# One group of small matmuls in place of two, three input buffers for it, and a later clamp in a convolution kernel

## Chip, core and metric

The kernel runs on one core of a Trainium2 chip. A core has five engines, each with its own queue that it works off in order: TensorE (PE in the profile; PEld is its weight load), VectorE (DVE), ScalarE (ACT), GpSimd (POOL) and SyncE (SP, which issues DMAs here). The metric is the time of one execution on the device in microseconds; smaller is better. All data are 32-bit floats.

## What is computed

The input x has 8 images of 256 channels and 64 x 64 pixels. Two layers follow each other, and each adds its result to its input. What matters here, cut from the reference:

```python
# layer 0, on the group-normalised x
x1, x2, x3 = _conv1x1(x, w1, b1), _conv1x1(x, w2, b2), _conv1x1(x, w3, b3)
...
h = jnp.concatenate([x1, x2u], axis=1)            # 320 channels: 32 + 9 shifts of 32
h = jax.nn.relu(_bn(h, bn1_g, bn1_b, bn1_m, bn1_v))
h = _conv1x1(h, cw1)                              # the inner conv: 320 -> 32
h = jax.nn.relu(_bn(h, bn2_g, bn2_b, bn2_m, bn2_v))
w = _conv1x1(h, cw2, cb2)                         # 9 weights per pixel and group
...
out = jnp.einsum('bgskhw,bgkhw->bgshw', x3u, w).reshape(B, OUT, H, W)
# layer 1, on the group-normalised result
att = jax.nn.softmax(jnp.einsum('bdn,bdkn->bnk', q, uk + upe[None]), axis=-1)
...
wts = jax.nn.softmax(wts, axis=2)                 # over 9 branches
hid = jax.nn.relu(_dwconv(xr, w1))
oc = _dwconv(hid, w2).reshape(b, kc2, C, h, w)
out_conv = jnp.sum(oc * wts.transpose(0, 2, 1, 3, 4), axis=1)
return rate1 * out_att + rate2 * out_conv
```

## The kernel before

An image is cut into 8 bands of 8 rows. The main loop runs over bands g; from g = 0 on it computes layer 1 of band g (image g // 8, band g % 8) and beside it pieces of layer 0 of bands that come later: the inner conv of band g + 11, the products of the nine pixel weights with the values (the taps) of band g + 10. Before that, in an opening of twelve bands, layer 0 runs alone. Layer 0 ends before the last bands: g = 0 to 52 contain an inner conv.

A band has 8 steps, s = 0 to 7, four for each half of the channels (ct = 0, 1; m = 0 to 3 in it). Step 6 is the seventh. Each step calls advance() six times. The order of instructions on each engine is the order in which the program issues them, and after(n, f) puts f off by n advances; a band is thus 48 places long, and step s begins at place 6s. Nothing else orders the work: an engine that has to wait holds up all that stands behind it in its queue.

In a step of layer 1 TensorE computes, among other things, scores (L750, tile sco, in even steps for two steps at once), the products of probabilities and values (L799, into the PSUM tile small), transposes (L787, tile ptp) and two groups of branch weights pf (L886). ACT turns each pf into exponentials ex (L891), and POOL adds up the ex tiles of a half band (L1106). There are three ex buffers, and pf, ptp, pv, pw, pk and pq share four PSUM buffers, so that a late addition on POOL keeps an exponential waiting, and that a matmul.

At a half band's end dynamic_sum closes the softmax over the nine branches: POOL adds the last two sums (L899, tile tot), adds 1 and limits the result to 1e37 (L902), VectorE takes the reciprocal in two halves through one buffer rec (L907), POOL multiplies (L908), then multiplies the depthwise result oc with it (L912) and adds that to xr (L913). oc itself is written by ACT (L879, in depthwise_end), at the end of step 3 or 7, and has two buffers.

The inner conv of a band (hidden_maps): ACT makes three inputs hid(0), hid(1), hid(2) of 512 columns (L424) in two buffers, at places 11, 16 and 25. The conv itself (L434) is twelve matmuls, four quarters of the band for each of the three inputs, each with 32 output rows; a 32-bit matmul leaves two records in the profile, so four matmuls are eight records. They go into a free part of the tile small: two inputs in step 4 (function one, place 24), whose sum ACT copies to SBUF (L446), and the third in step 6 (function two, place 36), after which VectorE adds the two (L450) and ACT applies scale, bias and ReLU (L441). In the opening (alone) the conv has a PSUM tile of its own, ph.

The taps: for each of nine taps VectorE makes a product prod (L483, two buffers, from the PSUM tile pw that L470 fills), and POOL adds it to xg (L491), 128 x 1024 elements each time.

Of the kernel before, what the change touches and what calls it, by code (L numbers as in the profile page):

```python
# [87 lines left out]
def conv_layers_kernel(ctx: ExitStack, tc: tile.TileContext, ins: dict, out: bass.AP):  # L88
# [102 lines left out]
    def layer1_loads():  # L191


        last = w1.tile([P, NCT, 1, C], F32, tag="oc", name="last")
        for f in late:
            f()
        nc.scalar.dma_start(out=last, in_=wfc_in[:, :, KK - 1 :])

        def first():
            nc.vector.tensor_scalar(wv, wv, rate1, None, ALU.mult)  # L200

        def difference(kt):
            nc.vector.tensor_sub(wfc[:, kt], wfc[:, kt], last[:, kt].to_broadcast([P, KK - 1, C]))

        return [first, lambda: difference(0), lambda: difference(1)]
# [205 lines left out]
    def hidden_maps(b, i, alone):  # L413

        im = images[b]
        hids = []
        h2 = h2n[i % 2][:, :, :W]

        def hidden(t):
            n = P if t == 0 else 96
            hid = w0.tile([P, R, W], F32, tag="hid", name=f"hid_{b}_{i}_{t}", bufs=2)
            nc.scalar.activation(  # L424
                hid[:n], im.x2[i][:n, t : t + R, :], AF.Relu, bias=bn1b[:n, t : t + 1], scale=bn1s[:n, t : t + 1]
            )
            hids.append(hid)

        def conv(home, first, last, start, stop):
            ph = home[:, 2 * P : 3 * P].rearrange("p (r c) -> p r c", r=SR)  # L430
            for t in range(first, last):
                n = P if t == 0 else 96
                for q in range(NQR):
                    nc.tensor.matmul(  # L434
                        ph[q * REL : (q + 1) * REL], c1[:n, t], hids[t][:n, q * SR : (q + 1) * SR],
                        start=(t == start), stop=(t == stop),
                    )
            return ph

        def relu(v):  # L440
            nc.scalar.activation(h2, v, AF.Relu, bias=bn2b, scale=bn2s)  # L441

        def one(home):
            ph = conv(home, 0, 2, 0, 1)
            after(1, lambda: hidden(2))
            after(2, lambda: nc.scalar.copy(h2, ph))  # L446

        def two(home):
            ph = conv(home, 2, 3, 2, 2)
            after(1, lambda: nc.vector.tensor_add(h2, ph, h2))  # L450
            after(3, lambda: relu(h2))

        hidden(0)
        after(3 if alone else 5, lambda: hidden(1))
        if alone:

            home = ps.tile([P, 4 * P], F32, tag="acc", name=f"ph_{b}_{i}")
            after(7, lambda: conv(home, 0, 2, 0, 2))
            after(8, lambda: hidden(2))
            after(12, lambda: after(4, lambda ph=conv(home, 2, 3, 0, 2): relu(ph)))  # L460
        return [two, one]

    def tap_weights(b, i, u, alone, at):

# [410 lines left out]

    def depthwise_end(b, i, ct, acc):

        oc = w1.tile([P, BAND], F32, tag="oc", name=f"oc_{b}_{i}_{ct}")
        nc.scalar.activation(oc, acc.rearrange("p r c -> p (r c)"), AF.Copy, scale=rate2)  # L879
        return oc  # L880

# [11 lines left out]
    def dynamic_sum(b, i, ct, ex, oc):  # L893

        tot = w1.tile([P, BAND], F32, tag="tots", name=f"tot_{b}_{i}_{ct}", bufs=1)
        xr = images[b].xr[i]

        engine = nc.vector if (b, i, ct) == (B - 1, NB - 1, NCT - 1) else nc.gpsimd
        engine.tensor_add(tot, ex[:, 1], ex[:, 0])  # L899


        engine.tensor_scalar(tot, tot, 1.0, 1.0e37, ALU.add, ALU.min)  # L902
        rec = w1.tile([P, BAND // 2], F32, tag="rec", name=f"rec_{b}_{i}_{ct}", bufs=1)

        def quotient(u):
            v = tot[:, u * BAND // 2 : (u + 1) * BAND // 2]
            nc.vector.reciprocal(rec, v)  # L907
            after(1, lambda: engine.tensor_mul(v, v, rec))  # L908

        def weigh():  # L910

            engine.tensor_mul(oc, oc, tot)  # L912
            engine.tensor_add(xr[:, ct], xr[:, ct], oc)  # L913
            if ct == NCT - 1:
                after(6, store)

        def store():
            nc.sync.dma_start(
                out=out[b].rearrange("(t p) n -> p t n", p=P)[:, :, i * BAND : (i + 1) * BAND], in_=xr
            )  # L920

        after(9, lambda: quotient(0))
        after(13, lambda: quotient(1))
        after(15, weigh)


    def beside(g, s):
# [96 lines left out]
    with tc.manual_schedule():  # L1024
# [21 lines left out]
        for g in range(-AHEAD, B * NB):  # L1046
            b, i = divmod(g, NB)
            for s in range(STEPS):
                ct, m = divmod(s, NT // 2)
                head, mid, end = beside(g, s)  # L1050
                if s == 1:
                    mid, maps = maps + mid, []
                steer(g, s)
                if g >= 0:
                    nm = f"{b}_{i}_{ct}_{m}"
                    weighted = []
                    if m % 2 == 0:
                        sco = score_tile(nm)
                        for e in range(2):
                            scores(b, i, ct, m + e, sco)  # L1060
                        small = small_tile(nm)
                        weighted, pending = weigh_steps(pending, small), []
                        if s == 0 and g + AHEAD < B * NB:
                            write = small_maps(*divmod(g + AHEAD, NB), small)
                            mid.append(lambda write=write: write((0,)))
                            maps.append(lambda write=write: write((1,)))
                        if s in (4, 6) and convs:
                            convs.pop()(small)
                        if before is not None:
                            pending.append((before[:-1], transposed(nm, before[-1])))  # L1070
                    prob, nmax = masked(nm, m, sco) if m % 2 == 0 else odd
                    for a, po in weighted:
                        add_values(*a, po)
                ahead = [f() for f in head]
                if g >= 0:
                    tot = exponentials(nm, prob, nmax)
                advance()
                for f in ahead:
                    if f:
                        f()  # L1080
                if g >= 0:
                    ex, exb = w1.tile([P, 2, BAND], F32, tag="ex", name=f"ex_{nm}", bufs=3), ex if m else None
                    branch_weights(b, i, ct, m, 0, ex)
                    if m % 2:
                        pending.append((before[:-1], transposed(nm, before[-1])))
                    if m in (0, 2):
                        todo = list(conv[0])
                    for _ in range(2):
                        todo.pop(0)()
                advance()  # L1090
                if g >= 0:
                    probabilities(prob, tot)
                rest = [f() for f in mid]
                advance()
                for f in rest:
                    if f:
                        f()
                if g >= 0:
                    for _ in range(2 if m % 2 == 0 else len(todo)):
                        todo.pop(0)()  # L1100
                    before = (b, i, ct, m, prob)
                advance()
                if g >= 0:
                    branch_weights(b, i, ct, m, 1, ex)
                    if exb is not None:
                        after(4, lambda ex=ex, exb=exb: nc.gpsimd.tensor_add(ex, ex, exb))  # L1106
                    if m == 1:
                        conv[1]()
                        conv = depthwise_middle(b, i, ct)
                    if m == NT // 2 - 1:  # L1110
                        oc = depthwise_end(b, i, ct, conv[1])
                        after(4, lambda a=(b, i, ct, ex, oc): dynamic_sum(*a))
                if s % 4 == 3 and 0 <= (g * NCT + ct + 1) < B * NB * NCT:
                    gn, cn = divmod(g * NCT + ct + 1, NCT)
                    conv = depthwise_begin(*divmod(gn, NB), cn)
                advance()
                for f in end:
                    f()
                if g >= 0 and m % 2 == 0:
                    odd = masked(f"{b}_{i}_{ct}_{m + 1}", m + 1, sco)  # L1120
                advance()
# [90 lines left out]
```

## Time and profile before

| what | value |
|---|---|
| median of 3 runs | 3856.01 us (3853.47 to 3856.48) |
| profiled execution | 3854.63 us |
| its span in the profile | 3852.8 us |
| granted TensorE clock, mean | 0.994 |
| HBM traffic | 127 GB/s over the span |
| inner conv, records of L434 in the bands | 1272, 270 to 297 ns each |
| limit L902 on POOL | 127 times, 1920 ns |
| limit L902 on VectorE (last half band) | once, 426 ns |
| copy L446, addition L450, ReLU L441 | 53 times each; 249, 280 and 483 ns |

An ordinary band takes 56.9 us, from one band's first score matmul to the next one's; the last image's bands take 49.6. In the timelines below a line has the start, the time, the engine, the source line, the operation, output and inputs, the shape and the count of merged instructions; in brackets stands how long the engine had been idle before it and what ended that wait. The lines with a stretch of time, such as 2405.50:2420.10, show its length and then, for each engine in the order PE, PEld, DVE, ACT, POOL, the busy time with the number of instructions, and last the clock, the share of the DMA engines and GB/s.

### The profile page before, as it was taken

What the parts mean: (1) busy time and instruction counts of PE and PEld (TensorE: products, weight loads), DVE (VectorE), ACT (ScalarE), POOL (GpSimd) and SP (SyncE); (2) the same over time, 40 slices, a digit from 0 to 9 for tenths busy, and PEclk for the clock granted to TensorE, in tenths of its full rate; (3) what the DMA queues carried; (4) which work ended last, traced back from release to release, by engine and by line L of the source; (5) the groups of instructions that cost most, each with busy time, mean ns of one, the idle gap of its engine ahead of it and who ended that gap; (6) DMA issues with size and microseconds to landing.
All of it is one profiled execution on the core that took longest, in us unless ns stands there. A gap on an engine that the chain in (4) does not pass through costs nothing.

```text
span 3852.8 us, 71646 instructions
## 1 busy us (share of the span) xinstructions
PE 3756.3 (97%) x24620; PEld 2109.9 (55%) x24620; DVE 3434.4 (89%) x7125; ACT 2809.2 (73%) x6770; POOL 3116.8 (81%) x2100
## 2 busy tenths in 40 slices
PE   6889999999999999999999999999999999999998
PEld 3445555555555555555555555555555555555554
DVE  6879999999999999899998999999999899978877
ACT  4457777777777777777777777777777777677776
POOL 4868888888897888888888888888888888855565
PEclk9999999999999999999999999999999999999999
DMA  8764544544444544544544544454544544232221
GB/s 247 210 177 128 142 118 129 151 126 118 133 135 131 145 123 115 148 135 127 136 116 142 142 125 120 126 149 125 136 115 117 138 119 114 74 97 78 79 67 37
DMA packets 438926, 490.14 MB, mean 127 GB/s; under 512 B 62016, under 2 KB 324256, under 8 KB 438304
## 3 DMA queue, kind: packets, MB, share of 16 engines
q1 hardware_dynamic: 421984, 469.79, 44.1%
q10 hardware_dynamic: 16576, 15.76, 1.3%
q8 instruction: 194, 3.18, 0.4%
q14 instruction: 172, 1.41, 0.1%
HBM read 343.76 MB, written 145.10 MB: 127 GB/s over the span
## 4 chain that ended last, share of the span: by engine, by line
PE 81%; POOL 10%; DVE 3%; DMA 2%; ACT 2%; issue 2%; SPq 1%; ACTq 0%; POOLq 0%; DVEq 0%
PE pf L886 39%; PE small L799 6%; PE ptp L787 6%; POOL xg L491 6%; PE pk L706 5%; PE pq L684 5%; PE sco L750 5%; PE p L375 5%; PE pv L601 5%; PE pw L470 2%; POOL ex L1106 2%; PE small L332 1%; DVE prod L483 1%; PE small L434 1%; DMA x<-x3n 1%
## 5 line engine op out<-in xcount | busy, mean ns | idle before, releaser
L886 PE MATMUL pf<-yp,c_wfc 128*128 128x512 f32 x4096 | 1916.8, 594 | 11.3 <-DVE prod L483 6.3
L491 POOL TENSOR_TENSOR xg<-xg,prod 128x1024 f32<-128x1024 f32 x549 | 1199.8, 2185 | 132.5 <-DVE prod L483 103.6
L886 PEld LDWEIGHTS pf<-yp,c_wfc 128*128 128x128 f32 x4096 | 739.6, 190 | 711.4 <-issue 654.7
L1106 POOL TENSOR_TENSOR ex<-ex,ex 128x1024 f32<-128x1024 f32 x384 | 908.8, 2367 | 68.5 <-ACT ex L891 65.0
L891 ACT ACTIVATE ex<-pf 128x512 f32<-128x512 f32 x1024 | 604.0, 590 | 347.9 <-PE pf L886 269.2
L843 DVE SCALAR_TENSOR_TENSOR acc<-yp,c_chan,acc 128x504 f32<-128x504 f32 (+3 forms) x1104 | 775.5, 702 | 63.2 <-ACT acc L834 42.8
L483 DVE SCALAR_TENSOR_TENSOR prod<-pw,c_par,x3q 128x1040 f32<-128x1040 f32 x576 | 732.7, 1294 | 107.9 <-PE pw L470 60.8
L869 DVE SCALAR_TENSOR_TENSOR acc<-hid,c_chan,acc 128x504 f32<-128x504 f32 (+3 forms) x1024 | 751.1, 733 | 18.1
L781 ACT ACTIVATE prob<-prob,tot 128x196 f32<-128x196 f32 x1024 | 412.9, 452 | 242.4 <-DVE tot L779 236.8
L772 ACT ACTIVATE prob<-prob,nmax 128x196 f32<-128x196 f32 x1024 | 458.2, 450 | 101.3 <-DVE nmax L764 101.2
L907 DVE RECIPROCAL rec<-tot 128x256 f32<-128x256 f32 x256 | 445.7, 1741 | 28.3 <-POOL tot L902 27.5
L789 ACT COPY pt<-ptp 112x512 f32<-112x512 f32 x511 | 295.9, 579 | 111.8 <-PE ptp L787 111.8
L764 DVE CUSTOM_DVE_ANT_0 prob<-sco,c_mask 128x196 f32<-128x196 f32 x1024 | 324.8, 355 | 31.0 <-PE sco L750 31.0
L787 PEld LDWEIGHTS ptp<-ident,prob 128*112 128x112 f32 x2044 | 227.3, 133 | 184.4 <-issue 132.7
L787 PE MATMUL ptp<-ident,prob 128*112 128x128 f32 x2044 | 319.5, 279 | 0.0
L908 POOL TENSOR_TENSOR tot<-tot,rec 128x256 f32<-128x256 f32 x254 | 185.8, 732 | 145.7 <-DVE rec L907 139.7
L799 PEld LDWEIGHTS small<-pt,vt 112*64 112x64 f32 x8144 | 258.6, 138 | 79.8 <-issue 60.5
L799 PE MATMUL small<-pt,vt 112*64 112x64 f32 x8144 | 294.2, 225 | 3.3 <-DMA vt<-vd 1.8
L601 PE MATMUL pv<-c_wv,yp 128*128 128x256 f32 x1056 | 253.5, 383 | 1.8 <-ACT yp L572 1.8
L902 POOL TENSOR_SCALAR tot<-tot 128x512 f32<-128x512 f32 x127 | 243.9, 1920 | 11.1
L470 PEld LDWEIGHTS pw<-h2n,c_c 128*128 128x128 f32 x1152 | 175.1, 191 | 139.9 <-issue 115.9
L375 PE MATMUL p<-xc,w3s 128*128 128x512 f32 x512 | 243.3, 598 | 0.0
(136 smaller groups left out, 4656.7 us busy)
## 6 DMA issues: line engine op xcount, KB each, us to landing
vt<-vd SPq DMA_DIRECT2D x512, 112.0 KB
x3q<-x SPq DMA_DIRECT2D x128, 264.0 KB
xc<-in_x SPq DMA_DIRECT2D x64, 512.0 KB
xg<-in_xg SPq DMA_DIRECT2D x64, 512.0 KB
yp<-x SPq DMA_DIRECT2D x128, 256.0 KB
xr<-x SPq DMA_DIRECT2D x64, 512.0 KB
out_x<-xr SPq DMA_DIRECT2D x64, 512.0 KB
xs<-in_x SPq DMA_DIRECT2D x57, 512.0 KB
```

What stands on the lines that cost most here:

```text
L483: nc.vector.scalar_tensor_tensor(prod[:, :, :RUN], pw[:, j, :RUN].unsqueeze(1).to_broadcast([P, SHARE, RUN]), par[:, PCB2 + k : PCB2 + k + 1],
L491: nc.gpsimd.tensor_add(im.xg[i], im.xg[i], rows(prod))
L601: nc.tensor.matmul(pv[:, g], yp[:, kt, r : r + 2].rearrange("p r c -> p (r c)"), wv[:, kt], start=(kt == 0), stop=(kt == NCT - 1),)
L772: nc.scalar.activation(prob[:, h, :NKEY], prob[:, h, :NKEY], AF.Exp, bias=nmax[:, h : h + 1], scale=-1.0, accum_out=tot[:, h : h + 1],)
L787: nc.tensor.transpose(ptp[:, h, ch], prob[:, h, ch * CHUNK : (ch + 1) * CHUNK], ident)
L799: nc.tensor.matmul(po[half[h], :, t * TQ : (t + 1) * TQ], im.vt[i + ch, m][:n, t, (2 * ct + h) * HD : (2 * ct + h + 1) * HD], pt[:n, h, ch ...
L843: nc.vector.scalar_tensor_tensor(o, yp[:, ct, ra + dr : rb + dr, ca + dc : cb + dc], chan[:, ct, CW1 + k : CW1 + k + 1], o, ALU.mult, ALU.add,
L869: nc.vector.scalar_tensor_tensor(o, hid[:, ra + dr : rb + dr, ca + dc : cb + dc], chan[:, ct, CW2 + k : CW2 + k + 1], o, ALU.mult, ALU.add,)
L886: nc.tensor.matmul(pf, wfc[:, kt, 2 * m + j, ct * P : (ct + 1) * P], images[b].yp[i][:, kt, PAD : PAD + R], start=(kt == 0), stop=(kt == N ...
L891: nc.scalar.activation(ex[:, j].rearrange("p (r c) -> p r c", r=R), pf, AF.Exp)
L907: nc.vector.reciprocal(rec, v)
L1106: after(4, lambda ex=ex, exb=exb: nc.gpsimd.tensor_add(ex, ex, exb))
```

## The change

The inner conv of a band is no longer split: all twelve matmuls are issued in step 6, accumulate in PSUM, and the ReLU reads them there one advance later. ACT's copy and VectorE's addition fall away. hid(2) is still made at place 25, but hid gets three buffers; to make room, oc (and the weights' tile that shares its tag) gets one. In the last band of each image, for the first half of the channels, the limit on tot is issued five advances later, the two reciprocals two and one advance later, and the product with oc one advance later. DMAs stay as and where they are.

```diff
-            hid = w0.tile([P, R, W], F32, tag="hid", name=f"hid_{b}_{i}_{t}", bufs=2)
+            hid = w0.tile([P, R, W], F32, tag="hid", name=f"hid_{b}_{i}_{t}", bufs=3)
...
-        def one(home):
-            ph = conv(home, 0, 2, 0, 1)
-            after(1, lambda: hidden(2))
-            after(2, lambda: nc.scalar.copy(h2, ph))
-
-        def two(home):
-            ph = conv(home, 2, 3, 2, 2)
-            after(1, lambda: nc.vector.tensor_add(h2, ph, h2))
-            after(3, lambda: relu(h2))
+        def inner(home):
+            ph = conv(home, 0, 3, 0, 2)
+            after(1, lambda: relu(ph))
...
+        else:
+            after(14, lambda: hidden(2))
+        return [inner]
...
-        oc = w1.tile([P, BAND], F32, tag="oc", name=f"oc_{b}_{i}_{ct}")
+        oc = w1.tile([P, BAND], F32, tag="oc", name=f"oc_{b}_{i}_{ct}", bufs=1)
...
-        engine.tensor_scalar(tot, tot, 1.0, 1.0e37, ALU.add, ALU.min)
+        def limit():
+            engine.tensor_scalar(tot, tot, 1.0, 1.0e37, ALU.add, ALU.min)
+
+        late = 2 if (i, ct) == (NB - 1, 0) else 0
+        if late:
+            after(5, limit)
+        else:
+            limit()
...
-        after(9, lambda: quotient(0))
-        after(13, lambda: quotient(1))
-        after(15, weigh)
+        after(9 + late, lambda: quotient(0))
+        after(13 + late // 2, lambda: quotient(1))
+        after(15 + late // 2, weigh)
...
-                        if s in (4, 6) and convs:
+                        if s == 6 and convs:
                             convs.pop()(small)
```

More of the change, by code (lines that the diff above doesn't have):

```diff
@@ L191, in layer1_loads @@
     def layer1_loads():
-        last = w1.tile([P, NCT, 1, C], F32, tag="oc", name="last")
+        last = w1.tile([P, NCT, 1, C], F32, tag="oc", name="last", bufs=1)
         for f in late:
@@ L460, in hidden_maps @@
             after(12, lambda: after(4, lambda ph=conv(home, 2, 3, 0, 2): relu(ph)))
-        return [two, one]
+        else:
+            after(14, lambda: hidden(2))
+        return [inner]
     def tap_weights(b, i, u, alone, at):
```

## The prediction

> **What bounds the kernel now.** I read the page's engine shares and chain of waits first, then one ordinary band (image 4, band 5, 2376.8 to 2433.7 us) cut into its four pairs of steps, then the timelines of single engines around the edited code.
>
> ```profile
> PE 3756.3 (97%) x24620; PEld 2109.9 (55%) x24620; DVE 3434.4 (89%) x7125; ACT 2809.2 (73%) x6770; POOL 3116.8 (81%) x2100
> PE 81%; POOL 10%; DVE 3%; DMA 2%; ACT 2%; issue 2%; SPq 1%; ACTq 0%; POOLq 0%; DVEq 0%
> 2391.40:2405.50 14.10, 14.10 (x89) 7.81 (x88) 13.82 (x28) 10.97 (x25) 12.68 (x9) 1.00 0.11 41
> 2405.50:2420.10 14.60, 14.60 (x115) 9.45 (x114) 13.77 (x26) 10.71 (x28) 14.28 (x8) 1.00 0.85 212
> ```
>
> TensorE (PE) looks like the only limit, but in steps 4 and 5 (the second of the two stretches, 2405.5 to 2420.1) GpSimd (POOL) is busy 14.28 of 14.60 us. So I followed POOL and those who wait for it.
>
> ```profile
> 2408.16 2.36 POOL L1106 TENSOR_TENSOR ex<-ex,ex 128x1024 f32<-128x1024 f32 x1
> 2410.48 4.44 POOL L491 TENSOR_TENSOR xg<-xg,prod 128x1024 f32<-128x1024 f32 x2
> 2414.88 2.37 POOL L1106 TENSOR_TENSOR ex<-ex,ex 128x1024 f32<-128x1024 f32 x1
> ...
> 2417.28 0.60 ACT L891 ACTIVATE ex<-pf 128x512 f32<-128x512 f32 x1 [1.91 <-POOL ex L1106]
> ...
> 2416.19 1.60 PEld L601 LDWEIGHTS pv<-c_wv,yp 128*128 128x128 f32 x8
> 2417.93 0.30 PEld L886 LDWEIGHTS pf<-yp,c_wfc 128*128 128x128 f32 x2
> ```
>
> POOL runs without a pause from 2395.40 (an xg addition of step 2) to 2417.25; the exponential of step 5 then starts at 2417.28, ends at 2417.88, and TensorE's next weight load (L886, second pf of step 5, whose PSUM buffer that exponential frees) comes 0.05 later. The load is some 0.1 later than the 0.02 it otherwise needs after the one before it, and its matmul starts only just on time. TensorE's own path has nothing left there: two chains tie. Matching every load with the wait that the built program gives it, this load stands 0.05 us behind ACT's exponential, and that 0.03 behind POOL, in 41 of the 53 bands that hold the changed conv; bands 3 (0.68) and 7 (0.12 to 0.16) of images 0 to 5 are the other twelve.
>
> The profile also holds a natural test. In image 6, band 5 is the first band with no inner conv; band 4 still has it:
>
> ```profile
> 3280.13 0.30 PEld L886 LDWEIGHTS pf<-yp,c_wfc 128*128 128x128 f32 x2 [0.90 <-ACT ex L891]
> ...
> 3334.01 0.30 PEld L886 LDWEIGHTS pf<-yp,c_wfc 128*128 128x128 f32 x2 [1.46 <-ACT ex L891]
> ...
> 3266.99 0.92 PE L750 MATMUL sco<-kb,qb 64*64 64x196 f32 x16
> 3282.27 0.92 PE L750 MATMUL sco<-kb,qb 64*64 64x196 f32 x16
> 3295.88 0.92 PE L750 MATMUL sco<-kb,qb 64*64 64x196 f32 x16
> ...
> 3320.88 0.92 PE L750 MATMUL sco<-kb,qb 64*64 64x196 f32 x16
> 3336.16 0.92 PE L750 MATMUL sco<-kb,qb 64*64 64x196 f32 x16
> ```
>
> Steps 4 and 5 last 15.28 in both bands: the conv's absence only lengthens the idle time from 0.90 to 1.46. Steps 6 and 7 do shrink, from 13.61 to 13.25 (the next score of band 5's successor is at 3349.40). Work in step 4 is hidden behind POOL; work in step 6 is paid in full.
>
> **What the Trainium skill says.** "Perfetto Trace Analysis", Optimization Strategy: the same gap repeating on an engine that should be saturated can mean that buffers ran out. Agrees: the late load of step 5 waits for a PSUM buffer, held up by the three ex buffers that POOL frees late. "TensorE: Matmul & The Clock Gate", Part 3, The mechanism: small matmuls at different tile positions overlap in the array. Agrees: eight L434 loads of 106 ns take 0.16 in all. "GPSIMD Engine Reference", 3.1: an elementwise addition is about twice as slow on GpSimd as on VectorE. Here the limit L902 is 1920 ns on POOL and 426 on VectorE, over four times.
>
> **The conv.** In the timeline of weight loads:
>
> ```profile
> 2392.23 1.01 PEld L799 LDWEIGHTS small<-pt,vt 112*64 112x64 f32 x32 [0.30 <-ACT ex L891]
> 2393.31 0.41 PEld L787 LDWEIGHTS ptp<-ident,prob 128*112 128x112 f32 x4
> ...
> 2406.39 1.01 PEld L799 LDWEIGHTS small<-pt,vt 112*64 112x64 f32 x32 [0.30 <-issue]
> 2407.47 0.38 PEld L434 LDWEIGHTS small<-hid,c_c 128*32 128x32 f32 x16
> 2408.04 0.40 PEld L787 LDWEIGHTS ptp<-ident,prob 128*112 128x112 f32 x4 [0.20 <-issue]
> ```
>
> From the end of L799 to the transposes L787: 0.07 without conv (step 2), 0.64 with 16 records (step 4), and 0.43 with 8 in step 6 (2421.93 to 2422.36). So the first piece costs 0.57, the second 0.36; eight records more are 0.21 to 0.22, the rest is the change of shape. After the change step 4 pays 0, step 6 pays 0.36 + 2 x 0.22 = 0.80: 0.44 more there, 0.57 less here, a net 0.13 per band for TensorE alone.
>
> In the 41 tied bands the 0.57 comes before the load that waits for POOL, and nothing in POOL's chain from step 2 to step 5 is edited or waits for the conv: it turns into idle time. The 0.44 comes after that load, and until step 5 of the next band I find no TensorE wait with less than 0.5 us to spare whose releaser moves against it: paid. 41 x 0.44 = +18.0. In band 3 the 0.57 fits into its 0.63: 6 x -0.13 = -0.8.
>
> With it go 53 ACT copies (249 ns, L446) and 53 VectorE additions (280 ns, L450). Both sit where their engine waits anyway: nothing. The ReLU L441 moves to just behind step 6's exponentials and delays the first ex of that step by 0.46; no TensorE load waits for that ex with under 0.7 to spare, and TensorE gets there 0.44 later: nothing.
>
> **Three hid buffers.** In the opening hid(2) waited for the first matmuls (ACT hid after PE ph: 10.4 us in 3 places). The chain passes that wait twice (54.99 and 199.88), 0.87 each with the issue: between -1.7 and 0; I take -0.9. In the bands the wait doesn't bind.
>
> **One oc buffer.** The write of oc (L879) now waits for POOL's addition L913 of the half band before. In the trace that addition ends before the write by 0.7 at the least in the first image, 1.1 or more later; example: 2377.88 against 2379.04. Step 6's extra 0.44 widens the narrow half. Zero; if it broke, behind it stand ACT's next acc copy L834 and the transposes' copy, a few tenths per band. The second wait is one queue instruction (17 ns for another of ACT's): nothing.
>
> **The limit in band 7** (images 0 to 5 have the taps beside it):
>
> ```profile
> 2532.03 1.92 POOL L902 TENSOR_SCALAR tot<-tot 128x512 f32<-128x512 f32 x1
> 2534.03 4.43 POOL L491 TENSOR_TENSOR xg<-xg,prod 128x1024 f32<-128x1024 f32 x2
> ...
> 2536.24 1.30 DVE L483 SCALAR_TENSOR_TENSOR prod<-pw,c_par,x3q 128x1040 f32<-128x1040 f32 x1 [0.50 <-POOL xg L491]
> ...
> 2535.90 0.40 PEld L787 LDWEIGHTS ptp<-ident,prob 128*112 128x112 f32 x4 [0.20 <-issue]
> 2537.60 0.30 PEld L886 LDWEIGHTS pf<-yp,c_wfc 128*128 128x128 f32 x2 [1.29 <-DVE prod L483]
> ```
>
> POOL's order becomes sum, xg, limit, xg, xg, ex, both products with the reciprocals. The first xg starts at 2531.94 and frees the prod buffer at 2534.1; the last prod then runs 2534.2 to 2535.4. Transposes to pf take 0.38 elsewhere, here 1.70: 1.32 lost. TensorE would want the load at 2536.28, shifted by -0.22 (what this band keeps of 0.57: 0.10 of slack and the 0.12 by which loads run ahead) and +0.44: 2536.50, later than prod. The stall goes: 6 x (-0.22 + 0.44 - 1.32) = -6.6. What is late next: the second reciprocal needs the one rec buffer and so waits for the first product, behind two xg and an ex, about 2543.5 instead of 2540.26. Behind it on VectorE are step 7's masks (some 0.7 later than 2545.07), then the exponentials; TensorE needs them for the transposes at 2553.7. Zero, at worst the 1.1 gained. In images 6 and 7 no taps stand beside it: zero.
>
> **Sum:** 18.0 - 0.8 - 6.6 - 0.9 = +9.7 on the profiled execution's 3854.63 (span 3852.8 and 1.8 around it) is 3864.3. The median stands 1.38 above that execution, so 3865.7.
>
> **Rivals.** (1) Not slower: POOL's chain ends 0.57 or more earlier in the ordinary bands, because a part of it is started by something that the change brings forward, and TensorE alone sets the time: 53 x -0.13, 6 x -1.32 and -0.9, -15.7, so 3840.3. For it speaks TensorE's 81% of the chain; against it the two bands of image 6. (2) The gain of band 7 only moves to another wait (the reciprocal behind POOL): 18.0 - 0.8 + 6 x 0.22 - 0.9 = +17.6, so 3873.6. For it: VectorE is 89% busy and in order; against: four microseconds to spare. (3) Half of the 0.44 disappears, because loads run ahead of matmuls after the stall: -9.0, so 3856.7. Against: in image 6 step 6 gave back its whole 0.36.
>
> **Chances.** Forecast 0.64, rival 1 0.13, rival 2 0.13, rival 3 0.10. The forecast's own range is 3861 to 3871: 0.05 per tied band is 2 us, the opening 0.9, band 7 another 1, and runs before differ by 3. The range 3856 to 3875 adds rivals 2 and most of 3; rival 1 stays out. A difference of 0.2% (7.7 us) is what measurement can tell from none: above 3863.7 lie three quarters of the forecast and rival 2, 0.61; below 3848.3 rival 1, 0.13; the rest 0.26.
>
> **What would show it.** Right: the load of step 5 idle 0.5 to 0.7 behind ACT's exponential in ordinary bands, steps 4 and 5 as long as before (14.5), steps 6 and 7 at 14.05 instead of 13.61, L434 in one group of 24, and no stall behind prod in band 7. Wrong: steps 4 and 5 shorter by half a microsecond, or ACT's oc waiting for POOL.

## The result, and the profile after

| | before | after |
|---|---|---|
| median | 3854.88 us (10 runs, 3849.93 to 3858.0) | 3865.21 us (10 runs, 3859.89 to 3869.82) |
| ratio | | 1.0026, 95% interval 1.0016 to 1.0035 |
| profiled execution (span) | 3854.63 (3852.8) us | 3869.82 (3867.7) us |
| mean granted TensorE clock in the profile | 0.994 | 0.991 |

The change makes the kernel 10.3 us slower. The profiled execution of after is the longest of its ten; the spans of the ten go from 3857.7 to 3867.7 us at mean clocks of 0.994 to 0.991. So the 14.9 us between the two profiles' spans are not yet the change's price: 1.8 of them lie in the opening, which does not repeat well (see the last section), and 13.1 behind it. Single stretches are compared instead, from one score matmul to the next, and the opening is left aside.

From the page of after: the engines' shares, the chain of waits by engine, and the group of the branch-weight matmuls (busy time and mean ns of one, then the idle time before them):

```profile
PE 3764.2 (97%) x24620; PEld 2115.7 (55%) x24620; DVE 3422.6 (88%) x7072; ACT 2804.8 (73%) x6717; POOL 3116.7 (81%) x2100
...
PE 61%; POOL 23%; DVE 6%; ACT 5%; issue 3%; DMA 2%; SPq 0%; ACTq 0%; POOLq 0%; DVEq 0%
...
L882 PE MATMUL pf<-yp,c_wfc 128*128 128x512 f32 x4096 | 1920.5, 595 | 16.7 <-ACT ex L887 15.6
```

The shares of busy time hardly move. The chain does: TensorE falls from 81% to 61%, POOL rises from 10% to 23%, although POOL does exactly the same work as before (2100 instructions, 3116.7 us). The chain passes through POOL because in most bands a matmul now really waits for it: the 16.7 us of idle time before pf are nearly all ended by ACT's exponential, whereas before it was 11.3 us, of which VectorE's prod ended 6.3. That 20 points of the chain move while the time moves by 0.3% fits two chains that end almost together.

An ordinary band (image 4, band 5) by pairs of steps, first steps 4 and 5, then 6 and 7; columns are length, then PE, PEld, DVE, ACT, POOL, clock, DMA. Before:

```profile
2405.54:2420.07 14.53, 14.53 (x111) 9.41 (x111) 13.73 (x26) 10.64 (x28) 14.21 (x8) 1.00 0.85 212
2420.07:2433.68 13.61, 13.61 (x90) 6.93 (x89) 12.43 (x27) 8.03 (x20) 13.37 (x11) 1.00 0.51 130
```

After:

```profile
2415.12:2429.66 14.54, 14.22 (x96) 9.04 (x95) 13.64 (x26) 10.43 (x27) 14.22 (x8) 1.00 0.86 212
2429.66:2443.71 14.05, 14.05 (x106) 7.37 (x105) 12.87 (x27) 8.11 (x20) 13.81 (x11) 1.00 0.49 131
```

Steps 4 and 5 lost the sixteen matmul records of the conv's first piece (the window's edges make it 15 here) and kept their length: PE is busy 14.22 of 14.54 us where it had been busy throughout. Steps 6 and 7 gained sixteen records and 0.44 us. The timelines of the weight loads, ACT and POOL of after show both places:

```profile
2424.46 2.37 POOL L1109 TENSOR_TENSOR ex<-ex,ex 128x1024 f32<-128x1024 f32 x1
...
2426.87 0.60 ACT L887 ACTIVATE ex<-pf 128x512 f32<-128x512 f32 x1 [2.49 <-POOL ex L1109]
...
2425.19 1.60 PEld L597 LDWEIGHTS pv<-c_wv,yp 128*128 128x128 f32 x8
2427.52 0.30 PEld L882 LDWEIGHTS pf<-yp,c_wfc 128*128 128x128 f32 x2 [0.72 <-ACT ex L887]
...
2430.51 1.01 PEld L795 LDWEIGHTS small<-pt,vt 112*64 112x64 f32 x32 [0.30 <-issue]
2431.59 0.60 PEld L434 LDWEIGHTS small<-hid,c_c 128*32 128x32 f32 x24
2432.38 0.41 PEld L783 LDWEIGHTS ptp<-ident,prob 128*112 128x112 f32 x4 [0.20 <-issue]
```

The load of step 5 stands idle for 0.72 us and starts 0.05 after the exponential ends, which itself waited for POOL's addition of the ex tiles. In bands 1, 2, 4 and 5 of images 0 to 5 this load idles 0.68 to 0.73, in band 6 1.02 to 1.06, in band 0 0.35 to 0.36. The conv is one group of 24 records; from the end of the L795 loads (2431.52) to the transposes it is 0.86. In step 6 of before it was 0.43:

```profile
2420.92 1.01 PEld L799 LDWEIGHTS small<-pt,vt 112*64 112x64 f32 x32 [0.30 <-issue]
2422.00 0.16 PEld L434 LDWEIGHTS small<-hid,c_c 96*32 96x32 f32 x8
2422.36 0.40 PEld L787 LDWEIGHTS ptp<-ident,prob 128*112 128x112 f32 x4 [0.20 <-issue]
```

Over all bands, after minus before by pairs of steps ("tied" are the bands in which POOL's chain and TensorE's path end together in step 5, or POOL's ends later):

| bands | steps 4, 5 | steps 6, 7 |
|---|---|---|
| 40 tied bands (images 0 to 5 without 3 and 7; image 6, 0 to 3) | 0.00 (-0.07 to +0.02; band 0 of images 1 to 6 -0.18 to +0.09, of image 0 -0.45) | +0.44 |
| band 3 of images 0 to 5 | -0.58 | +0.43 |
| band 7 of images 0 to 5 | -0.22 | -0.87 |
| image 6, band 4 | -0.56 | +0.45 |
| image 6, band 5 | -0.59 | 0.00 |
| last score matmul to the end of the span | | 25.46 before, 28.42 after |

Steps 0 to 3 stay within 0.01, but for band 0 of image 0, right behind the opening: there steps 2 and 3 are 1.43 longer, and the band as a whole is 1.2 longer. Band 7 alone gains in steps 6 and 7; there the limit was moved. The timelines of after around its step 6 (image 4):

```profile
2541.12 1.27 POOL L895 TENSOR_TENSOR tot<-ex 128x512 f32<-128x512 f32 x1
2542.34 2.18 POOL L487 TENSOR_TENSOR xg<-xg,prod 128x1024 f32<-128x1024 f32 x1
2544.61 1.92 POOL L899 TENSOR_SCALAR tot<-tot 128x512 f32<-128x512 f32 x1
...
2544.56 1.30 DVE L479 SCALAR_TENSOR_TENSOR prod<-pw,c_par,x3q 128x1040 f32<-128x1040 f32 x1 [1.65 <-POOL xg L487]
...
2546.59 0.40 PEld L783 LDWEIGHTS ptp<-ident,prob 128*112 128x112 f32 x4 [0.20 <-issue]
2546.97 0.30 PEld L882 LDWEIGHTS pf<-yp,c_wfc 128*128 128x128 f32 x2
```

The limit now stands behind the first xg. The product ends at 2545.86, over 1 us before the load of L882 comes up, and that load no longer carries a bracket: it follows the transposes after 0.38, where it had stood idle for 1.29 behind prod.

The last line of the table is the very end of the program. Before, VectorE and POOL there:

```profile
3826.37 1.75 DVE L907 RECIPROCAL rec<-tot 128x256 f32<-128x256 f32 x1
3828.36 0.36 DVE L764 CUSTOM_DVE_ANT_0 prob<-sco,c_mask 128x196 f32<-128x196 f32 x1 [0.25 <-PE sco L750]
...
3831.58 1.73 DVE L907 RECIPROCAL rec<-tot 128x256 f32<-128x256 f32 x1
...
3833.39 0.73 POOL L908 TENSOR_TENSOR tot<-tot,rec 128x256 f32<-128x256 f32 x1 [2.14 <-DVE rec L907]
...
3836.78 4.79 POOL L1106 TENSOR_TENSOR ex<-ex,ex 128x1024 f32<-128x1024 f32 x2
```

After:

```profile
3840.30 0.36 DVE L760 CUSTOM_DVE_ANT_0 prob<-sco,c_mask 128x196 f32<-128x196 f32 x1 [1.91 <-PE sco L746]
...
3841.89 1.74 DVE L910 RECIPROCAL rec<-tot 128x256 f32<-128x256 f32 x1
3843.55 1.46 DVE L865 SCALAR_TENSOR_TENSOR acc<-hid,c_chan,acc 128x504 f32<-128x504 f32 x2
...
3845.04 1.53 DVE L865 SCALAR_TENSOR_TENSOR acc<-hid,c_chan,acc 128x504 f32<-128x504 f32 x2
3846.47 1.75 DVE L910 RECIPROCAL rec<-tot 128x256 f32<-128x256 f32 x1
...
3848.30 0.73 POOL L911 TENSOR_TENSOR tot<-tot,rec 128x256 f32<-128x256 f32 x1 [3.86 <-DVE rec L910]
...
3851.69 4.77 POOL L1109 TENSOR_TENSOR ex<-ex,ex 128x1024 f32<-128x1024 f32 x2
...
3851.78 0.69 ACT L875 ACTIVATE oc<-acc,c_rowp 128x512 f32<-128x512 f32 x1 [0.15 <-POOL xr L916]
```

Before, the first reciprocal ran while VectorE waited for the last scores; the masks then waited only 0.25. After, the masks wait 1.91 with nothing in that gap, the first reciprocal comes behind them, and one more pair of depthwise operations stands before the second one. The last score matmul starts at 3827.38 before and 3839.31 after; the second reciprocal follows it by 4.20 before and by 7.16 after, POOL's last two additions by 9.40 and 12.38. These 3.0 us reach the end undiminished: the closing operations on VectorE begin when POOL's last addition is done. It is also the one place where ACT's oc waits for POOL (0.15).

### The profile page after: what moved, and what is told of

Its sections match the earlier page's. It is cut to its first block, busy times and chain, and to the rows that moved or that the text cites. A ratio compares the mean times of both kernels' runs of the same rounds, so it can differ in the third digit from the quotient of the medians.

```text
span 3867.7 us, 71658 instructions
## 1 busy us (share of the span) xinstructions
PE 3764.2 (97%) x24620; PEld 2115.7 (55%) x24620; DVE 3422.6 (88%) x7072; ACT 2804.8 (73%) x6717; POOL 3116.7 (81%) x2100
## 4 chain that ended last, share of the span: by engine, by line
PE 61%; POOL 23%; DVE 6%; ACT 5%; issue 3%; DMA 2%; SPq 0%; ACTq 0%; POOLq 0%; DVEq 0%
PE pf L882 29%; POOL xg L487 12%; POOL ex L1109 7%; PE small L795 5%; PE sco L746 4%; PE p L375 4%; PE ptp L783 4%; PE pq L680 3%; PE pk L702 3%; DVE prod L479 2%; PE pv L597 2%; PE pw L466 1%; PE small L332 1%; POOL oc L915 1%; ACT ex L887 1%
## 5 line engine op out<-in xcount | busy, mean ns | idle before, releaser
L882 PE MATMUL pf<-yp,c_wfc 128*128 128x512 f32 x4096 | 1920.5, 595 | 16.7 <-ACT ex L887 15.6
L882 PEld LDWEIGHTS pf<-yp,c_wfc 128*128 128x128 f32 x4096 | 739.2, 190 | 725.3 <-issue 661.2
L795 PEld LDWEIGHTS small<-pt,vt 112*64 112x64 f32 x8144 | 258.5, 138 | 79.6 <-issue 60.5
L795 PE MATMUL small<-pt,vt 112*64 112x64 f32 x8144 | 294.0, 225 | 3.4 <-DMA vt<-vd 1.8
L899 POOL TENSOR_SCALAR tot<-tot 128x512 f32<-128x512 f32 x127 | 243.9, 1920 | 11.1
L357 POOL COPY x<-x 32x8 f32<-32x8 f32 x64 | 12.1, 189 | 296.4 <-ACT x L347 296.4
```

The source lines that it names most:

```text
L795: nc.tensor.matmul(po[half[h], :, t * TQ : (t + 1) * TQ], im.vt[i + ch, m][:n, t, (2 * ct + h) * HD : (2 * ct + h + 1) * HD], pt[:n, h, ch ...
L882: nc.tensor.matmul(pf, wfc[:, kt, 2 * m + j, ct * P : (ct + 1) * P], images[b].yp[i][:, kt, PAD : PAD + R], start=(kt == 0), stop=(kt == N ...
```

## The experiments

Theory: in steps 2 to 5 of an ordinary band POOL's chain and TensorE's own path end together, so taking work out of step 4 gives nothing, and work put into step 6 is paid in full. The first rival: the two places are alike, and the loss comes from something else in the change (buffers, the single oc, VectorE's order). The second: the limit moved in band 7 only shifts its stall.

### The parts of the change

**The joined conv without the later limit** (edit of after):

```diff
-        late = 2 if (i, ct) == (NB - 1, 0) else 0
+        late = 0
```

> The changed kernel without the later limit: one conv group in step 6, three hid buffers, one oc buffer. Theory (POOL's chain hides step 4, step 6 is paid): each ordinary band keeps its +0.44, bands 3 their -0.14; in band 7 of images 0 to 5 the stall of 1.31 is back and swallows what the conv adds there, so band 7 is as before; the end is as in the kernel before. 39 x 0.44 - 6 x 0.14 - 0.7 (bands 4 and 5 of image 6, as measured) = +15.6 against before: about 3870.5. Rival (the conv alone only saves TensorE 0.13 a band, and the loss came from the limit): 3848.

Measured: 3868.05 us (5 runs, 3866.44 to 3869.71), ratio to before 1.0037 (1.0024 to 1.0049). By bands: +0.44 in the tied ones, -0.58 and +0.43 in band 3, about -0.22 and +0.20 in band 7, the two bands of image 6 as in after, the end at 25.46 as before. So the loss of steps 6 and 7 and the gains of image 6 belong to the conv and its buffers, which are taken alone below; the end does not. The medians of the series differ by 15.2, where 15.6 was expected.

**The later limit alone, in images 0 to 5** (edit of before, the later limit as in the change but under a condition):

```diff
+        late = 2 if (i, ct) == (NB - 1, 0) and b < B - 2 else 0
```

> The kernel before with the later limit alone, and only in images 0 to 5, where taps stand beside it. Theory: the stall of 1.31 behind prod goes in six bands and nothing else moves: -7.9 against before, about 3847. Rival (the stall only moves to the reciprocals and step 7's masks): 0 to -2, about 3854.

Measured: 3846.38 us (20 runs), ratio 0.9982 (0.9976 to 0.9989). Steps 6 and 7 of the six bands are 1.30 to 1.34 shorter, no other band moves by more than 0.06, the end takes 25.47. The rival of the shifted stall falls: the wait is gone, and nothing takes its place.

**The later limit alone, in all eight images** (edit of before):

```diff
+        late = 2 if (i, ct) == (NB - 1, 0) else 0
```

> The kernel before with the later limit in all eight images' last bands. Theory: six bands with the taps gain 1.32 each (7.9, as when the limit alone is moved there), and the last half band's end comes 3.0 later by the second reciprocal behind POOL's first product: -4.9, 3848.6; the stretch from the last score matmul to the end goes from 25.5 to 28.4. Rival (the longer end needs the single oc buffer or the joined conv): the end stays at 25.5 and the time is 3846.

Measured: 3848.7 us (21 runs), ratio 0.9988 (0.9982 to 0.9995). The six bands gain 1.30 to 1.34 again, and the end takes 28.42. So the 3.0 us at the end come from the limit's edit by itself; neither the single oc buffer nor the conv is needed. The number was as expected, but the mechanism named there was not: in this run and in after VectorE is busy without a pause from the first reciprocal to the second, and POOL's first product (in after 3843.71 to 3844.44) is long done. The second reciprocal is late by its place in VectorE's order, not by the rec buffer.

**The whole change with the later limit in images 0 to 5 only** (edit of after):

```diff
-        late = 2 if (i, ct) == (NB - 1, 0) else 0
+        late = 2 if (i, ct) == (NB - 1, 0) and b < B - 2 else 0
```

> The changed kernel with the later limit left out in the last two images. Theory (in the last half band the later reciprocals delay POOL's last two ex additions and with them the end): the last stretch, from the last score matmul to the end, takes 25.4 again instead of 28.4, and nothing else changes: -3.0 against the changed kernel, about 3862. Rival (the longer end in the profile is TensorE's slower clock there, half speed for 17.5 us instead of 10.5): still 28, about 3865.

Measured: 3861.47 us (18 runs), ratio to before 1.0021 (1.0014 to 1.0028). All bands but the very first are as in after, the end takes 25.46 instead of 28.42. The medians differ from after's by 3.7, the two ratios by 0.0005 (1.9 us); the 3.0 of the end lies between. The rival named for this run falls as well: TensorE's mean clock over the last stretch is lower here (0.77) than in before (0.83), and both take 25.46.

**The buffers alone** (edit of before: three hid buffers, one oc buffer; the weights' tile that shares oc's tag gets one too):

```diff
-            hid = w0.tile([P, R, W], F32, tag="hid", name=f"hid_{b}_{i}_{t}", bufs=2)
+            hid = w0.tile([P, R, W], F32, tag="hid", name=f"hid_{b}_{i}_{t}", bufs=3)
...
-        oc = w1.tile([P, BAND], F32, tag="oc", name=f"oc_{b}_{i}_{ct}")
+        oc = w1.tile([P, BAND], F32, tag="oc", name=f"oc_{b}_{i}_{ct}", bufs=1)
```

> The kernel before with the buffer edits alone: three hid buffers, one oc buffer; conv split as before, limit as before. Theory: nothing in any band (the oc write never waits), 0 to 1.7 less in the opening: 3852 to 3853.5. Rival (the single oc buffer costs): ACT's oc is idle behind POOL's addition in half bands, a few tenths in each of 64 bands, 3865 or more.

Measured: 3854.39 us (13 runs, 3847.26 to 3859.1), ratio 1.0003 (0.9994 to 1.0011). That is 0.9 above the range that was expected, well within an interval that is 6.5 us wide. Band 0 of images 1 to 5 moves by +0.06 to +0.08 in steps 4 and 5, 0.4 in all, and band 0 of image 0 by +1.2; no other by more than 0.06. The same first band moves by -0.9 to 0.0 in the runs that leave the buffers alone and by -1.5 to +1.2 in those that have them, so its +1.2 is not put down to the buffers. They are not the loss of steps 6 and 7 or of the end. Whether the opening gains up to 1.7 can't be told.

### The tie with POOL, from both sides

**Without the first piece** (edit of before; step 4 then has no conv and no copy on ACT):

```diff
-            ph = conv(home, 0, 2, 0, 1)
             after(1, lambda: hidden(2))
-            after(2, lambda: nc.scalar.copy(h2, ph))
```

> The kernel before without the first piece of the inner conv: step 4's matmuls and ACT's copy are left out, the third input is added to what stood in the buffer. Theory: 0.57 of TensorE's work per band is free under POOL's chain, except in band 3 (-0.57, six times): the idle time of step 5's load grows by 0.57 and the time falls by 3.4 to 4.5, about 3850. Rival (TensorE's work counts wherever it stands): 53 x -0.57 = -30, about 3824.

Measured: 3851.06 us (13 runs), ratio 0.9996 (0.9987 to 1.0004). That is 2.4 less than before, where 3.4 to 4.5 was expected; the interval goes from 5.0 less to 1.5 more. The 16 records cost 0.57 us on TensorE, yet behind band 0 of image 0 only band 3 (-0.57) and steps 4 and 5 of band 7 (-0.22, which its stall in step 6 takes back) get shorter. The same load of step 5 in the timeline of weight loads, and steps 4 and 5 of the band, in this kernel:

```profile
2418.20 0.30 PEld L884 LDWEIGHTS pf<-yp,c_wfc 128*128 128x128 f32 x2 [0.69 <-ACT ex L889]
```

```profile
2405.84:2420.34 14.50, 14.21 (x95) 9.04 (x95) 13.64 (x26) 10.43 (x27) 14.18 (x8) 1.00 0.89 213
```

Work taken from step 4 turns into 0.69 of idle time, just as after the change.

**Without the second piece** (edit of before; step 6 then has no conv and no addition on VectorE):

```diff
-            ph = conv(home, 2, 3, 2, 2)
-            after(1, lambda: nc.vector.tensor_add(h2, ph, h2))
```

> The kernel before with the third input's four matmuls and VectorE's addition left out of step 6 (the branch weights then lack that part of the conv's sum; step 4's piece stays). Theory (step 6 pays in full, step 4 is covered by POOL): 0.36 less in steps 6 and 7 of every one of the 53 bands, with at most 0.2 of it lost in band 7 of images 0 to 5, 47 to 53 x 0.36 = 17 to 19 us: about 3836. Rival (the two places are alike, both are hidden behind POOL or in TensorE's slack): as the kernel before without step 4's piece, 3851. Rival (the 0.36 is mostly the change of shape and comes back at the next group): 3845.

Measured: 3839.13 us (5 runs), ratio 0.9962 (0.9949 to 0.9974). Steps 6 and 7 are 0.35 to 0.36 shorter in 46 bands, in all 53 but the six bands 7, which stay, and band 4 of image 0 (0.14). The sum of that, about 17, is at the lower end of the expected 17 to 19, a little more than the 14.4 between the medians and inside their interval (10 to 20). Steps 6 and 7 of the same band as above:

```profile
2404.90:2418.15 13.25, 13.25 (x81) 6.77 (x81) 12.10 (x26) 8.03 (x20) 13.01 (x11) 1.00 0.48 129
```

Half as many records as in the run before, and several times the gain: the places are not alike.

**POOL relieved, in after**: the copy of the last band's rows into kb (L670, 0.54 us) stands in POOL's chain of steps 2 to 5; for the second half of the channels it goes to ACT.

```diff
-                nc.gpsimd.tensor_copy(kb[:, : 2 * PAD], im.kb[i - 1, ct][:, R:])
+                (nc.scalar.copy if ct else nc.gpsimd.tensor_copy)(kb[:, : 2 * PAD], im.kb[i - 1, ct][:, R:])
```

> The changed kernel with one copy of POOL's chain (kb rows of the second channel half, 128x420, 0.53 us, step 2) moved to ACT. Theory: POOL's chain from step 2 to step 5 is 0.5 shorter, the idle time of step 5's load falls from 0.7 to about 0.2, and the 39 tied bands become 0.45 to 0.5 shorter: -18, about 3847. Rival (what was lost is TensorE's own work in step 6): unchanged, 3865.

Measured: 3847.32 us (17 runs), ratio to before 0.9983 (0.9976 to 0.999), where after has 1.0026. Steps 4 and 5 of the tied bands are 0.43 to 0.53 shorter than in after (those of band 0 of an image are not: no such copy stands in its chain), steps 6 and 7 as in after. The load and the windows of the same band:

```profile
2411.75 0.30 PEld L882 LDWEIGHTS pf<-yp,c_wfc 128*128 128x128 f32 x2 [0.21 <-ACT ex L887]
```

```profile
2399.86:2413.89 14.03, 14.03 (x96) 9.04 (x95) 13.65 (x26) 10.41 (x27) 13.79 (x7) 1.00 0.83 209
```

The idle time falls from 0.72 to 0.21, what POOL gave up.

**POOL relieved, in before** (the same edit of before):

> The kernel before with the kb copy of step 2 on ACT. Theory (before, POOL's chain and TensorE tie, so a shorter chain brings nothing in ordinary bands): only band 6 (-0.33), band 7's stall (-0.48, six times each) and bands 4 and 5 of image 6 (-0.5 each) gain: -5.9, about 3847. Rival (POOL's chain sets every band): 41 x -0.48, about 3833.

Measured: 3846.83 us (21 runs), ratio 0.9984 (0.9977 to 0.999). The ordinary bands gain nothing (0.00); the 6.7 us come from band 6 (-0.41), band 7 (about -0.48), bands 4 and 5 of image 6 (-0.76 and -0.64) and the end (-0.3): 6 x 0.89 + 1.4 + 0.3 = 7.0. In the ordinary band the load now has no wait at all, and the steps are as long as ever:

```profile
2413.75 0.41 PEld L886 LDWEIGHTS pf<-yp,c_wfc 128*128 128x128 f32 x2
```

```profile
2401.47:2416.00 14.53, 14.53 (x112) 9.50 (x111) 13.74 (x26) 10.65 (x28) 14.29 (x7) 1.00 0.84 201
```

That settles the tie. Relieving TensorE alone gives nothing (no first piece), relieving POOL alone gives nothing (this run), relieving both gives half a microsecond in every tied band whose chain holds the copy (the run before this one).

### A better place

**The joined conv in step 4**, where POOL covers 0.57 of its 0.80 (edit of the version with the limit in images 0 to 5):

```diff
-            after(14, lambda: hidden(2))
+            after(11, lambda: hidden(2))
...
-                        if s == 6 and convs:
+                        if s == 4 and convs:
```

> The changed kernel with the one conv group in step 4 instead of step 6 (hid(2) three advances earlier), and the later limit only in images 0 to 5. Theory: the group of 24 costs 0.80 in step 4, where TensorE just ties with POOL's chain, and step 6 pays nothing: +0.22 and -0.36 against the kernel before, -0.14 in an ordinary band; where TensorE idled for POOL in step 5 (band 0 by 0.1, band 6 by 0.33) the 0.22 is free; the stall of band 7 is gone. 53 x -0.14 - 2.0 - 7.9 = -17 against before, about 3837. Rival (the place doesn't matter, only the group's size): as with step 6, 3862.

Measured: 3839.72 us (5 runs, 3834.86 to 3843.07), ratio 0.9968 (0.9955 to 0.998). Against before, steps 4 and 5 are 0.20 to 0.22 longer in ordinary bands and steps 6 and 7 are 0.36 shorter; band 0 of the later images loses 0.3 to 0.6 in steps 4 and 5, which was not foreseen and has not been traced. It makes up about 3 us, what the run stays behind the 17 that were expected. The load of step 5 has no wait, and the band's two windows are:

```profile
2394.44:2409.18 14.74, 14.74 (x119) 9.72 (x118) 13.73 (x26) 10.79 (x28) 14.42 (x8) 1.00 0.84 209
2409.18:2422.43 13.25, 13.25 (x81) 6.77 (x80) 12.30 (x26) 7.65 (x19) 13.01 (x11) 1.00 0.51 131
```

**The same with the kb copy on ACT**:

> The same, with the kb copy of step 2 on ACT as well. Theory: TensorE alone sets the ordinary bands in step 4's version, so 0.5 less in POOL's chain brings nothing there; only band 6 (0.1 each) and bands 4 and 5 of image 6 (0.5 each) gain: -1.5 against the version in step 4, about 3835. Rival (POOL still sets the bands): -0.5 in 40 bands, 3817.

Measured: 3835.17 us (5 runs, 3828.41 to 3836.61), ratio 0.9952 (0.9939 to 0.9964). It beats both kernels: 18.3 us less than before in the same series, an interval of 0.36 to 0.61%. Ordinary bands are as in the run before it; band 6, band 0 and the two bands of image 6 gain.

## Why the prediction was right, and where it was not

The predicted time, 3865.7, is met (3865.21), and so is the difference (+9.7 against +10.3). That it is met to half a microsecond is luck: two terms were missed that partly cancel, a third can't be resolved, and the interval of the difference is 7 us wide. The main term and its mechanism are right.

- **The conv.** Right in place and size. Step 6 was to pay 0.44 more, and all 41 tied bands pay 0.43 to 0.45 there; steps 4 and 5 give something back only in band 4 of image 6 (-0.56) and in band 0 of images 0 and 4 (-0.45 and -0.18). The tie with POOL that makes step 4's piece free is shown from both sides by the four runs on it. The natural test in image 6 had pointed the right way. Of the rivals, the first (POOL's chain ends earlier, TensorE alone sets the time) needs steps 4 and 5 to shrink, and they don't; the third (half of the 0.44 disappears) falls with the 0.44.
- **Band 3.** -0.15 each against -0.13.
- **ACT's copy, VectorE's addition, the moved ReLU: "nothing".** Right in the tied bands, where steps 6 and 7 show the conv's 0.44 and no more. Not in image 6's bands 4 and 5, which together end 1.1 us earlier than predicted (-0.12 and -0.59 measured, +0.44 and 0 predicted). The buffers alone do not do it (nothing there), nor does leaving out the first piece (nothing there). From step 5 of one band to step 5 of the next these two bands take 0.13 and 0.14 less in after (step 6 longer by 0.44), 0.25 and 0.22 less without the second piece (step 6 shorter by 0.36), and 0.33 and 0.16 less with the conv in step 4 (again shorter by 0.36). VectorE's 0.28 is missing in all three, and the length of step 6 shows little. That fits a loop from band to band that runs through VectorE and POOL there and not through TensorE: step 6 may grow at no cost, and VectorE's addition counts. That this is the loop is argued from these three runs; none isolated it.
- **Three hid buffers: -0.9 in the opening.** Open. The buffers alone make 3854.39 against 3853.5, with an interval from -2 to +4 us.
- **One oc buffer: zero.** Right, but for 0.4 us that the two buffer edits cost together in band 0 of five images, and for band 0 of image 0, which can't be resolved; ACT's wait for POOL appears only in the last half band, and there as a consequence of the late limit.
- **The limit in band 7 of images 0 to 5.** Right: -1.09 per band against -1.10, and the second reciprocal, expected 9.9 us after the score matmul, came 10.2 after it (2554.08 against 2543.86), and TensorE lost nothing by it: steps 6 and 7 change by the conv's 0.44 and the stall's 1.31 alone. The second rival falls.
- **The step that was missed** is "In images 6 and 7 no taps stand beside it: zero". It looked for taps, since they make the gain, and not for what the moved reciprocals themselves stand behind. The first reciprocal of the last half band but one had filled a gap in which VectorE waited for the scores; moved, it leaves that gap empty and delays the second reciprocal, POOL's product and the additions behind it by 3.0 us, with nothing left to hide it. The limit alone and the change without it in images 6 and 7 show this amount.

Put together without the opening: 40 x 0.44 = 17.6, band 3 -0.9, band 7 -6.5, image 6 -0.7, the end +3.0, in all +12.5; the two profiles themselves differ there by 13.1, with the very first band's odd 0.8. The prediction had +10.6. The medians say +10.3, with an interval from 6 to 13.5; whether the opening makes up the difference is open.

## What to carry over

Where two engines' chains end together, the price of an operation depends on which side of the meeting point it stands: find that point by the smallest wait in the timeline, and put what has to be moved ahead of it, where the other chain covers it. Relieving one of two tied chains shows nothing, which is no proof that it doesn't matter; relieve both. And a reordering that is made for the steady state has to be priced separately in the last pieces of the loop, where the cover is gone and a delay of a few microseconds goes straight to the end.

## What the hardware showed that was not expected

The opening does not repeat to better than some microseconds. In the profiles of the kernels that keep before's opening the first score matmul of layer 1 comes between 231.3 and 238.0 us, in those with after's between 226.1 and 235.4. TensorE's clock was granted at half speed for 48.0 us in the profile of before and for 68.7 in that of after: in the opening, for 6.8 us in band 0 of image 0, and at the very end (from 8.4 us before the end of the span in before, from 15.2 in after). In the other profiles, too, 3.4 to 10.2 us at half speed fall into that first band, which may be why it does not repeat; no run isolates it. The bands between run at full clock, and what an edit leaves alone there repeats from profile to profile mostly to 0.02 us and nearly always to 0.06. An effect of a microsecond can be measured in a band, and not in the opening.

Sixteen or twenty-four records of the same small matmuls are not twice or three times eight: 8 took 0.36, 16 took 0.57 and 24 took 0.80 us, so about 0.22 go with each eight and about 0.14 with the group itself, an estimate from these three. That the 0.14 is the change of shape between groups was not tested. Joining two groups saves it once per band, but only on TensorE's own path.

How much slower POOL is than VectorE depends on the operation. The addition of two 128x512 halves (L899 before) takes 1.27 us on POOL and 0.69 on VectorE, the limit 1.92 and 0.43: 1.8 times against 4.5.
